# The last block's recurrences at half pace beside a preparation

## The chip, the cores and the metric

The kernel runs on one core of a Trainium2 chip. The metric is device time in microseconds of one execution; a kernel's figure is the median of its runs. A profiled execution gives the trace: PE is TensorE, DVE VectorE, ACT ScalarE, POOL GpSimd, SP the engine that issues most DMAs.

## The reference, cut to what matters

The reference is a network of four blocks on x of 16 x 64 tokens of 256 features, each block with a cross attention into a context of 1024 keys per batch, a sequence layer, and a feed-forward layer, all with a layer norm ahead and a residual sum behind. The change is in the last block (L3), whose three layers are:

```python
# cross attention: 8 heads of 64
q = (x @ Wq).reshape(B, Nq, HEADS, DIM_HEAD)
...
attn = jax.nn.softmax(sim, axis=-1)
...
# state space layer
combined = x @ in_proj_w
u, x_gate = jnp.split(combined, 2, axis=-1)
u_c = conv(u)                                  # 3 taps, by channel
u = jax.nn.silu(u_c + conv_b)
delta, b, c = jnp.split(u @ x_proj_w, ...)
delta = jax.nn.softplus(delta @ dt_proj_w + dt_proj_b)
h = jnp.exp(d_t[:, :, None] * a) * h + d_t[:, :, None] * b_t[:, None, :] * u_t[:, :, None]
y_t = jnp.einsum('bds,bs->bd', h, c_t)         # h: 512 channels x 16 states
...
y = (y + u * D_param) * jax.nn.silu(x_gate)
return y @ out_proj_w
# dense layer: weights of +1 and -1, widths 1024, 1024, 256
h = s0 * _conn_dense(k0, jnp.concatenate([x, -x], axis=-1))
h = s1 * _conn_dense(k1, jax.nn.relu(h) * 2)
return s2 * _conn_dense(k2, jax.nn.relu(h) * 2)
```

(The convolution's call and some shapes are shortened.)

## The kernel before, in words

The 1024 tokens lie as 8 tiles of 128 rows in SBUF (`xs`). The last block, `L3`, weaves three layers together. The attention, `heads64`, goes through 32 steps (tile, batch of the pair, group of four heads) and calls `breathe` four times per step, which in this block is `ssm.go()`. When a tile's attention is added to `xs`, `finished` raises `ssm.ready`. Then the dense layer runs four passes over two tiles each; each pass is a generator whose yields give a share, and `ssm.go(share, hurry=2)` is called at each of them, but for the first two of the first pass. Ahead of each pass stands a loop that calls `go` until those two tiles have come out of the state space layer (`while ssm.done < i + 2`).

The state space layer works on four chunks of 256 tokens (two tiles), each in two generators:

- `prepare(k)`: layer norm, projection (`win`), the convolution's taps on DVE (L1944, L1949), Silu, the b and c rows (`bc`, written to DRAM as `bcs`), delta (L1971 to L1976) and delta times u, written to DRAM as `dus`. It has 14 yields. Some yield `WAIT`, which ends the hurry of that call. A preparation begins when its two tiles have left the attention, and if it is at most two chunks ahead of `done`.
- `items(k)`: the recurrences. There are eight slots (four blocks of 128 channels, two halves), each of four beats. A beat forms the decays on ACT (two activations, L2020), the inputs on DVE (L2026), the recurrence on DVE (L2030, one scan along 512 elements) and the product with c (L2033), in one of six `x` buffers. One beat into the next slot, `add_up` sums the slot's states on PE (L2054, 16 matmul records); every second slot then is multiplied by the gate on DVE (L2060, L2061). After the eight slots come the last sum, the output by `wout` and its sum into `xs` (L89), and `done` rises. So a chunk has 32 beats and three more turns.

`fetch` loads a slot's `rep` buffers (four in all) from `dus`, one slot ahead, in eight DMAs on SP's queue; `bc_rep` (one buffer) comes from `bcs` in eight. The context tiles of the attention and the outputs use SP's queue too.

`go` sets the pace: it resumes the preparation once (or `hurry` times), then adds `share * s.rate` to a credit of at most `2 * s.rate`, and resumes the recurrences once for each whole unit. The rate is 1.1 in the attention and 1.4 in the dense passes. Chunk 0's preparation lies in steps 10 to 13 of the attention, chunk 1's in 18 to 21, chunk 2's in 26 to 29, and chunk 3's in the first dense pass.

The order on PE is the order of the program (`manual_schedule`); on the other engines a scheduler sets it when the program is built, with the tiles' dependences. On each engine instructions run in that order.

Of the kernel before, what the change touches and what calls it, by code (L numbers as in the profile page):

```python
# [42 lines left out]
class Net:  # L43
# [1832 lines left out]
    def state_space(self):  # L1876
# [4 lines left out]
        s = SimpleNamespace(ready=0, done=0, rate=1.1, credit=0.0, prepared=0, started=0)  # L1881
# [183 lines left out]
        def go(share=1.0, hurry=1):  # L2065


            for _ in range(hurry):
                if s.prep is None and s.prepared < NC and s.ready >= 2 * s.prepared + 2 and s.prepared <= s.done // 2 + 1:
                    s.prep = prepare(s.prepared)  # L2070
                got = None if s.prep is None else next(s.prep, s)
                if got is s:
                    s.prepared += s.prep.gi_code is prepare.__code__
                    s.prep = None
                if got is WAIT:
                    break
            if s.work is None and s.started < s.prepared:
                s.work = items(s.started)
                s.started += 1
            self.spare_dve = s.work is not None  # L2080
            s.credit = min(s.credit + share * s.rate, 2 * s.rate)
            while s.work is not None and s.credit >= 1:
                s.credit -= 1
                if next(s.work, s) is s:
                    s.work = None

        def more(i):
            s.ready = i + 1

        s.go, s.more, s.first = go, more, first  # L2090
        s.x = rooms(self.sb, "x", 6)
        s.rep = rooms(self.sb, "rep", 4)
# [333 lines left out]
```

## Time and profile before

| What | us |
|---|---|
| median of 3 runs (lowest, highest) | 2947.67 (2939.41, 2950.96) |
| the profiled execution | 2943.51 |
| its span | 2941.7 |
| PE, DVE, ACT busy in it | 2681.1, 1466.4, 1043.0 |
| 2700 to 2784 (first dense pass): PE, DVE busy | 73.5, 55.4 |
| 2784 to 2834 (second dense pass): PE, DVE busy | 48.3, 44.3 |

The last block's attention begins at about 2017 us and ends at about 2700; the four dense passes fill the rest. The profile's groups name a line, an engine, the output and input tiles, and a count; an instruction issued by a helper bears the helper's line (L69 is the matmul helper, L179 the transpose, L89 the sum into `xs`). A stretch's table gives each engine's busy time within it; its length less PE's busy time is PE's wait.

### The profile page before, as it was taken

To read this page: it belongs to the slowest core of one execution; us is meant where nothing else is said; L and a number is where in the kernel's file an instruction comes from. 1 tells how busy PE (TensorE), PEld (TensorE's weight loads), DVE (VectorE), ACT (ScalarE), POOL (GpSimd) and SP (SyncE) were. 2 spreads that over 40 slices of the span, in tenths; PEclk is the share of its full clock that TensorE was granted. 3 is DMA by queue.
4 is the path that set the end of the run, shared out by engine and by line. 5 is a ranking of instruction groups with operands and counts; after the bars stand their busy time and mean duration, and the time that the engine had idled before them with its cause. 6 is when DMAs were issued, how large, how long until landed. Compare 5 with 4: busy or idle time off the path is not lost. (4 is left out here: it accounts for less than half of the span.)

```text
span 2941.7 us, 42834 instructions
## 1 busy us (share of the span) xinstructions
PE 2681.1 (91%) x16972; PEld 1973.5 (67%) x16972; DVE 1466.4 (50%) x3120; ACT 1043.0 (35%) x2350; POOL 306.1 (10%) x407
## 2 busy tenths in 40 slices
PE   7887898999999898989999998898998898888999
PEld 3556785566666586867777776795766666666777
DVE  2555113666666653234444444323446656658593
ACT  1322121555555441223333322122334455455330
POOL 1111232100000011310101001101001000000000
PEclk9897998999999997989999999899999999999999
DMA  8512772111010113811111111552213213121110
GB/s 235 167 49 81 279 270 73 35 30 36 27 37 23 41 37 137 298 53 45 56 56 45 44 54 61 214 218 75 69 43 87 70 42 94 54 73 29 57 45 8
DMA packets 79221, 253.57 MB, mean 86 GB/s; under 512 B 15151, under 2 KB 26954, under 8 KB 69290
## 3 DMA queue, kind: packets, MB, share of 16 engines
q1 hardware_dynamic: 59562, 165.01, 18.1%
q0 software_dynamic: 13312, 80.28, 8.0%
q10 hardware_dynamic: 6144, 5.51, 0.5%
q8 instruction: 135, 2.21, 0.3%
q14 instruction: 68, 0.56, 0.1%
HBM read 233.80 MB, written 14.82 MB: 85 GB/s over the span
## 5 line engine op out<-in xcount | busy, mean ns | idle before, releaser
L223 DVE TENSOR_REDUCE nmx<-sc 128x1 f32<-128x1024 f32 x264 | 311.9, 1219 | 223.8 <-PE sc L508 132.8
L225 ACT ACTIVATE p<-sc,nmx 128x1024 f32<-128x1024 f32 x264 | 294.6, 1116 | 312.8 <-DVE nmx L223 312.2
L508 PE MATMUL sc<-ctxT,qp 128*128 128x512 f32 (+1 forms) x1024 | 357.0, 603 | 0.0
L508 PEld LDWEIGHTS sc<-ctxT,qp 128*128 128x128 f32 (+1 forms) x1024 | 139.5, 190 | 154.8 <-issue 152.6
L69 PE MATMUL halves<-ctx,pT 128*128 128x192 f32 x1024 | 188.0, 339 | 9.4 <-DVE xs L89 4.0
L69 PEld LDWEIGHTS halves<-ctx,pT 128*128 128x128 f32 x1024 | 175.7, 200 | 12.3 <-DVE xs L89 4.5
L69 PE MATMUL misc<-ctx,pT 128*128 128x192 f32 x1024 | 177.6, 327 | 0.5 <-DVE qT L473 0.5
L235 PE MATMUL ps_t<-ident,p 128*128 128x128 f32 x1088 | 147.6, 278 | 25.2 <-ACT p L225 17.6
L69 PEld LDWEIGHTS misc<-ctx,pT 128*128 128x128 f32 x1024 | 166.3, 191 | 2.2 <-DVE qT L473 1.0
L2020 ACT ACTIVATE da<-rep,al 128x252 f32<-128x252 f32 x256 | 115.1, 498 | 117.8 <-DVE x L2030 101.1
L2030 DVE TENSOR_TENSOR_SCAN x<-da,x 128x512 f32<-128x512 f32 x128 | 152.9, 1220 | 3.4 <-ACT da L2020 2.8
L237 ACT COPY pT<-ps_t 128x512 f32<-128x512 f32 x182 | 104.3, 585 | 140.3 <-PE ps_t L235 138.4
L235 PEld LDWEIGHTS ps_t<-ident,p 128*128 128x128 f32 x1088 | 127.4, 143 | 39.2 <-ACT p L225 22.4
L235 PE MATMUL misc<-ident,p 128*128 128x128 f32 x1024 | 138.3, 280 | 13.4 <-ACT p L225 6.3
L235 PEld LDWEIGHTS misc<-ident,p 128*128 128x128 f32 x1024 | 110.7, 141 | 39.7 <-ACT p L225 14.4
L160 POOL TENSOR_TENSOR ln_rs<-ln_ve,nhalf 128x1 f32<-128x1 f32 x80 | 45.7, 576 | 691.7 <-DVE ln_ve L158 552.7
L237 ACT COPY pT<-misc 128x512 f32<-128x512 f32 x128 | 75.0, 586 | 115.4 <-PE misc L235 115.0
L69 PE MATMUL ps_h<-r,w 128*128 128x256 f32 x512 | 113.4, 381 | 0.0
L69 PE MATMUL gu<-dT,wa 128*128 128x128 f32 (+1 forms) x864 | 104.8, 280 | 3.9 <-ACT dT L64 2.4
L239 DVE COPY pT<-misc 128x512 f32<-128x512 f32 x128 | 88.3, 690 | 38.8 <-PE misc L235 28.2
L69 PEld LDWEIGHTS ps_h<-r,w 128*128 128x128 f32 x512 | 96.6, 190 | 15.9 <-issue 2.5
L69 PEld LDWEIGHTS gu<-dT,wa 128*128 128x128 f32 (+1 forms) x864 | 98.3, 185 | 11.2 <-ACT dT L64 4.8
(478 smaller groups left out, 4479.1 us busy)
## 6 DMA issues: line engine op xcount, KB each, us to landing
ctx<-in_ctx SPq DMA_DIRECT2D x48, 768.0 KB
ctxT<-in_ctxT SPq DMA_DIRECT2D x48, 512.0 KB
w<-in_L2f_W SPq DMA_DIRECT2D x24, 1024.0 KB
rep<-dus SPq DMA_DIRECT2D x256, 64.0 KB
ctxT<-in_ctxT SPq DMA_DIRECT2D x16, 768.0 KB
ctxT<-in_ctxT SPq DMA_DIRECT2D x96, 128.0 KB
ys<-yb ACTq DMA_DIRECT2D x40, 128.0 KB
bc_rep<-bcs SPq DMA_DIRECT2D x32, 128.0 KB
```

Source lines behind the costliest of these rows:

```text
L69: self.nc.tensor.matmul(out, lhsT, rhs, start=n == 0, stop=n == len(pairs) - 1)
L160: nc.gpsimd.tensor_tensor(rs, ve, self.nhalf, ALU.pow)
L223: self.nc.vector.tensor_reduce(nmx, sc, AX.X, ALU.max, negate=True)
L225: self.nc.scalar.activation(p, sc, AF.Exp, bias=nmx, accum_out=sums)
L235: self.nc.tensor.transpose(ps[:, u, :], p[:, at : at + 128], self.ident)
L237: self.nc.scalar.copy(pT[:, 4 * g : 4 * g + 4, :], ps)
L239: self.nc.vector.tensor_copy(pT[:, 0:4, :], ps)
L508: nc.tensor.matmul(sc[u][:, bass.ts(kh, 512)], qp[n][par][rows, h : h + 2, :].rearrange("p h q -> p (h q)"), ctx[0][rows, at], start=n == ...
L2020: nc.scalar.activation(da[:, g, :, 1:], now[j][:, 0, :].rearrange("p (b s) -> p b s", s=S)[:, :, 1:], AF.Exp, scale=al[:, col : col + 1],)
L2030: nc.vector.tensor_tensor_scan(flat, da.rearrange("p g b s -> p (g b s)"), flat, 0.0, ALU.mult, ALU.add)
```

## The change

A call of `go` adds half as much credit while a preparation is in progress, if the rate is at most 1.1. That is so in the attention alone: there a call adds 0.55 in place of 1.1 while `s.prep` is set. The dense passes have rate 1.4, and there a call adds what it added. Nothing else is touched.

```diff
             self.spare_dve = s.work is not None
-            s.credit = min(s.credit + share * s.rate, 2 * s.rate)
+
+            s.credit = min(s.credit + share * s.rate * (1 if s.prep is None or s.rate > 1.1 else 0.5), 2 * s.rate)
             while s.work is not None and s.credit >= 1:
```

From L2082 on the changed kernel's line numbers are one higher.

## The prediction

> **What bounds the kernel now.** I read the page's busy row first: TensorE (PE) is busy for 91% of the span, so what counts is where it waits. The change touches only the last block, so the table of stretches comes next. Its columns are length, then busy time (instructions) of PE, PEld, DVE, ACT and POOL, then granted clock, DMA share and GB/s.
>
> ```profile
> PE 2681.1 (91%) x16972; PEld 1973.5 (67%) x16972; DVE 1466.4 (50%) x3120; ACT 1043.0 (35%) x2350; POOL 306.1 (10%) x407
> ```
>
> ```profile
> 2101.00:2164.00 63.00, 61.92 (x347) 45.91 (x346) 26.87 (x60) 20.03 (x49) 3.77 (x5) 1.00 0.18 55
> 2164.00:2253.00 89.00, 81.23 (x425) 60.40 (x424) 40.86 (x84) 38.04 (x80) 6.81 (x11) 0.98 0.24 68
> 2253.00:2345.00 92.00, 75.85 (x410) 53.83 (x411) 64.02 (x99) 45.06 (x116) 5.53 (x5) 0.93 0.25 73
> 2345.00:2442.00 97.00, 86.42 (x480) 62.04 (x477) 55.76 (x92) 49.15 (x113) 7.43 (x11) 0.98 0.23 65
> 2442.00:2533.00 91.00, 78.18 (x433) 56.35 (x434) 64.23 (x98) 46.78 (x121) 0.55 (x1) 0.96 0.25 74
> 2533.00:2634.00 101.00, 88.79 (x475) 63.23 (x474) 50.71 (x88) 46.37 (x107) 4.65 (x9) 0.95 0.20 59
> ...
> 2834.00:2891.50 57.50, 55.91 (x290) 43.44 (x290) 44.58 (x68) 15.43 (x35) 0.55 (x1) 1.00 0.10 28
> ```
>
> Rows one to six are the attention, four steps each: one with neither preparation nor recurrences, one with a preparation alone, then recurrences alone, both, recurrences alone, both. PE waits 1.1, 7.8, 16.2, 10.6, 12.8 and 12.2 us in them. The last row is the third dense pass with recurrences beside it: PE waits 1.6 of 57.5 us although DVE has 44.6 us of work. So recurrences lie almost free beside the dense layers, and cost PE waits beside the attention.
>
> Then the timeline of DVE where it runs recurrences without interruption, and that of PE around the last dense pass:
>
> ```profile
> 2794.57 2.33 DVE L2030 TENSOR_TENSOR_SCAN x<-da,x 128x512 f32<-128x512 f32 x2
> 2796.82 1.26 DVE L2033 TENSOR_TENSOR x<-x,bc_rep 128x512 f32<-128x512 f32 x2
> 2798.01 1.28 DVE L2026 TENSOR_TENSOR x<-rep,bc_rep 128x512 f32<-128x512 f32 x2
> 2799.21 2.33 DVE L2030 TENSOR_TENSOR_SCAN x<-da,x 128x512 f32<-128x512 f32 x2
> ```
>
> ```profile
> 2877.69 7.17 PE L69 MATMUL halves<-w,r 128*128 128x256 f32 x32
> 2885.44 1.92 PE L2054 MATMUL halves<-x,stack 128*32 128x256 f32 x16 [0.58 <-DVE xs L2159]
> 2887.29 3.72 PE L69 MATMUL halves<-w,ug 128*128 128x256 f32 x16
> ...
> 2895.04 8.86 PE L69 MATMUL ps_h<-hT,w 128*128 128x256 f32 x32 [0.46 <-ACT hT L64]
> ```
>
> A pair of recurrence beats returns after 2799.21 - 2794.57 = 4.64 us: one beat is 2.32 us of DVE. Before the fourth dense pass, PE ends the third (2884.86), sums the last slot (1.92), multiplies by `wout` (3.72), and starts the fourth at 2895.04: nothing of chunk 3's recurrences is left by then.
>
> **The change part by part.** *How many beats move.* A preparation lives for 14 calls of `go` (its 14 yields). Two of them, of chunks 1 and 2, lie in the attention while recurrences run. Each loses 14 x 0.55 = 7.7 beats, 15.4 together. Following the credit call by call, the attention ends with 87 beats done before and 71 after: 16 fewer. Preparation 0 has no recurrence beside it, and preparation 3 falls into the dense passes, at rate 1.4, which the condition leaves alone. Nothing takes the 16 back: in the dense passes the rate is the same, so the lag is carried to the end. Before the fourth pass, the loop that waits for `done` has two beats left in the kernel before (the last sum and the output), and 14 recurrences more after. The built program says the same: after the third pass's two residual updates (now L2160) DVE has 14 triples L2026, L2030, L2033, and PE four sums in a row.
>
> *The tail.* PE has nothing else there. 14 x 2.32 = 32.5 us; the two pairs L2060/L2061 amid them cost 0.40 + 0.34 (from one start to the next at 2840.65) each, 1.5 us. Half of the last sum, 0.96 us, must follow the last beat; it replaces a whole one, 1.92. Together 32.5 + 1.5 + 0.96 - 1.92 = **+33.0**. DVE works in order and the residual updates stand ahead of the 14, so the dense pass's 12.9 us of DVE slack (57.5 - 44.6) is not used for them. What waits behind: both normalizations, the transposes, and the whole fourth pass. Bounds: +24 if four beats are nearer than the order says; +42 if each of the four slots waits some 2 us for its `rep` transfers (eight issues of about 0.4 us and a landing of 1.73 us in the chain make 5 us, within a slot's 9.3, so I take none).
>
> *PE after the gap.* Here a row and a rule differ in size. PE's timeline shows a sum of 2.84 us where others take 1.92, after PE stood 2.60 us:
>
> ```profile
> 2586.89 2.38 PE L69 MATMUL halves<-ug,w 128*32 128x256 f32 x8 [2.60 <-ACT onT L64]
> 2589.71 2.84 PE L2054 MATMUL halves<-x,stack 128*32 128x256 f32 x16 [0.45 <-ACT bc L1962]
> ```
>
> So a pause costs about 0.5 + 0.9 = 1.4 us. The Trainium skill ("TensorE: Matmul & The Clock Gate", Part 1) has the clock at half after an idle window of some 3.4 us, and back after some 3.4 us of work: in the tail PE stands about 7 us between sums, so half a sum and the output (0.96 + 3.72) run at half speed for up to 3.4 us, +1.7. The fourth pass's first layer is slow already (8.86 against 7.17 elsewhere). Row +1.4, rule +1.7, both if the next layer suffers more: I take **+2** (0 to 4).
>
> *The start of the third pass.* Chunk 2's output stood a whole pass ahead of its reader; now it comes one sum before it, in the built order, with chunk 3's first beats among its normalizations. First, L2026 of chunk 3 waits for `bc_rep`, one buffer, free only after chunk 2's last L2033: eight issues of 0.42 us on SP and 1.7 us landing, 5.1 us. L2061, which the output's matmuls need, stands behind that L2026 on DVE. Then four scans (1.13 each), three L2026 and four L2033 (0.6 each) stand ahead of the second normalized tile: 8.7 us. Walking both queues, PE ends the second pass some 12.8 us after chunk 2's last L2033 and gets the third pass's first input at 19.8; less two transposes of 0.4 it waits 6.2 us, where it now waits 2.1 (1.68 and 0.46 before 2834.96). With the clock, **+5** (2 to 8).
>
> *The first and second pass.* One more sum in the second, **+1.85**; the first carries 17 beats instead of 13 on DVE, 9 us more into 28.6 us of its idle time there (2700 to 2784: 84 - 55.4), some of it when PE waits for the preparation: **+1** (-1 to 3).
>
> *What the attention gains.* Four sums leave PE: 4 x 1.85 = **-7.4**, certain, as PE is the bound there. The waits: in the stretches with both, PE waits 10.6 and 12.2 us against 7.8 with a preparation alone, so about seven beats fewer in two of them save some 2 us. In those with recurrences alone it waits 16.2 us for some 17 beats, near 0.9 each; they too lose about seven, because chunk 0's and chunk 1's sums and outputs now fall there, and these bring waits of their own (1.75 us for xs at 2428). I take **-6** (0 to -14). Two outputs of 3.6 us only change their stretch. SP's queue: the slower `rep` loads stand in front of context loads there, but those are two steps ahead; nothing (0 to +3).
>
> *Sum.* 33.0 + 2 + 5 + 1.85 + 1 - 7.4 - 6 = **+29.5**. The profiled execution took 2943.5 us (span 2941.7), so 2973; it lies 4.2 below the median of the runs, 2947.7, from which a new median is 2977.
>
> **The rivals.** (1) *DVE works ahead.* The gap of 14 beats shrinks since DVE's 12.9 us of slack in the third pass swallow five: +29.5 - 11.6 = +18, 2966. For it: the slack is there. Against it: the order of DVE puts the residual updates first.
>
> (2) *The attention is bound by DVE there, and the change pays.* If each of the 16 beats blocked a softmax or an average for its full 2.32 us, the attention would give back 37.1 + 7.4 = 44.5 us against 42.9 lost: 2946; it decides from (42.9 - 7.4) / 16 = 2.2 us per beat. For it: in the second stretch with recurrences alone DVE is busy 64 of 91 us, and PE's waits there end on `on` L522 and `p` L225. Against it: with a preparation beside them, the four steps take 97 and 101 us, with the preparation alone 89; less one output (3.6), 12 to 14 beats cost about 6 us, 0.46 each, which is their sums and no more. All of PE's waits in those two stretches are 22.8 us.
>
> (3) *Transfers pace the tail.* SP loads four `rep` buffers in order, and the third pass's outputs stand among them: at +9 more, 2986.
>
> That the change does nothing is excluded: the built order differs by these beats.
>
> **How the numbers follow.** Forecast 0.72, own range 2964 to 2991; rival 1 0.12, rival 2 0.05, rival 3 0.11. The range of 2958 to 2993 leaves out rival 2 and the ends of the others. A measurement of this kernel tells about 0.5% (15 us) from no change, that is 2962. Slower: all but a few of the forecast's and rival 3's cases and half of rival 1's, 0.88; within: 0.08; faster: most of rival 2, 0.04.
>
> **What would show it.** In the changed kernel: 14 L2030 in a row between the third pass's last residual update and the fourth pass, about 34 us, with PE busy there for four sums only; a wait of 5 to 7 us of PE before the third pass; the attention shorter by 10 to 17 us. It is wrong if PE's waits in the attention fall by over 20 us, if the 14 beats run before the residual updates, or if a slot in the tail takes clearly more than 9.3 us.

## The result and the profile after

The changed kernel takes 2982.43 us (median of 6 runs, 2978.33 to 2985.51) where the kernel before takes 2944.91 (also 6 runs): a ratio of 1.0132, 95% interval 1.0118 to 1.0146, or 37.5 us more. The forecast was 29.5 us more, 2977, in a range of 2958 to 2993. The profiled execution took 2978.33 us, its span 2976.6.

The busy row of the changed kernel's page: the same instructions, PE 18 us busier.

```profile
PE 2699.3 (91%) x16972; PEld 1986.3 (67%) x16972; DVE 1464.7 (49%) x3120; ACT 1042.5 (35%) x2350; POOL 304.7 (10%) x407
```

The table of stretches (length, then busy time and instructions of PE, PEld, DVE, ACT, POOL, granted clock, DMA share, GB/s), of the changed kernel: the four steps beside chunk 1's preparation, the four beside chunk 2's, the third dense pass, and what lies between it and the fourth.

```profile
2356.70:2454.10 97.40, 87.31 (x460) 64.66 (x458) 47.90 (x79) 49.80 (x115) 3.50 (x7) 0.95 0.23 68
2542.30:2635.20 92.90, 81.76 (x426) 60.43 (x425) 49.58 (x79) 48.91 (x112) 3.49 (x7) 0.96 0.19 55
2832.30:2881.60 49.30, 49.28 (x240) 39.71 (x240) 36.46 (x52) 16.17 (x36) 0.00 (x0) 0.97 0.15 41
2881.60:2929.90 48.30, 24.59 (x101) 11.13 (x101) 38.68 (x59) 10.64 (x24) 1.10 (x2) 0.61 0.10 25
```

The same four of the kernel before, cut at the same instructions:

```profile
2360.80:2457.40 96.60, 85.95 (x475) 62.43 (x474) 55.11 (x92) 49.91 (x116) 5.21 (x9) 1.00 0.24 72
2545.90:2647.00 101.10, 88.14 (x458) 63.63 (x457) 57.02 (x89) 50.74 (x117) 2.95 (x6) 0.95 0.22 64
2835.00:2884.90 49.90, 49.86 (x256) 39.40 (x256) 40.84 (x59) 15.05 (x34) 0.00 (x0) 1.00 0.11 29
2884.90:2895.00 10.10, 6.45 (x36) 4.21 (x36) 4.49 (x13) 0.74 (x2) 1.10 (x2) 1.00 0.04 13
```

The last rows are the result: between the third and the fourth pass 10.1 us have become 48.3, with DVE busy for 38.7 of them, and PE's clock at 0.61. The stretch beside chunk 2's preparation is 8.2 us shorter, the one beside chunk 1's 0.8 longer. These two must be read with one thing in mind: in the kernel before, chunk 0's output (3.6 us of PE) lies in the stretch beside chunk 1's preparation and chunk 1's output in the one beside chunk 2's; in the changed kernel each comes one stretch later. Without the outputs, and so for like work, the stretch beside chunk 2's preparation became about 4.6 us shorter, of which one sum less is 1.85, and the one beside chunk 1's about 4.4 us longer.

What happens in the 48.3 us is in PE's timeline of the changed kernel:

```profile
2874.51 7.07 PE L69 MATMUL halves<-w,r 128*128 128x256 f32 x32
2882.15 1.96 PE L2054 MATMUL halves<-x,stack 128*32 128x256 f32 x24 [0.58 <-DVE xs L2160]
2886.71 1.06 PE L2054 MATMUL halves<-x,stack 128*32 128x256 f32 x2 [2.60 <-DVE x L2033]
2890.75 1.91 PE L2054 MATMUL halves<-x,stack 128*32 128x256 f32 x8 [2.98 <-DVE x L2033]
...
2917.88 2.51 PE L2054 MATMUL halves<-x,stack 128*32 128x256 f32 x8 [2.12 <-DVE x L2033]
2920.32 5.52 PE L69 MATMUL halves<-w,ug 128*128 128x256 f32 x16
...
2929.86 8.86 PE L69 MATMUL ps_h<-hT,w 128*128 128x256 f32 x32 [0.46 <-ACT hT L64]
```

PE sums states in pieces and waits at each for DVE's L2033, as a pair of beats ends every 4.64 us. In DVE's own timeline the residual updates stand first, as the order of the built program had it, and then 14 beats follow to 2918.43:

```profile
2881.62 0.48 DVE L2160 SCALAR_TENSOR_TENSOR xs<-halves,sc,xs 128x256 f32<-128x256 f32 x1 [1.27 <-PE halves L69]
2883.24 0.69 DVE L2026 TENSOR_TENSOR x<-rep,bc_rep 128x512 f32<-128x512 f32 x1 [1.14 <-PE halves L2054]
...
2901.98 0.48 DVE L2060 SCALAR_TENSOR_TENSOR v<-ug,vecs,halves 128x256 f32<-128x256 f32 x1 [0.81 <-PE halves L2054]
...
2917.16 1.27 DVE L2033 TENSOR_TENSOR x<-x,bc_rep 128x512 f32<-128x512 f32 x2
```

### The profile page after: what moved, and what is told of

Read it like the earlier page. It is cut to its first block, busy times and chain, and to the rows that moved or that the text cites. A ratio compares the mean times of both kernels' runs of the same rounds, so it can differ in the third digit from the quotient of the medians.

```text
span 2976.6 us, 42824 instructions
## 1 busy us (share of the span) xinstructions
PE 2699.3 (91%) x16972; PEld 1986.3 (67%) x16972; DVE 1464.7 (49%) x3120; ACT 1042.5 (35%) x2350; POOL 304.7 (10%) x407
## 5 line engine op out<-in xcount | busy, mean ns | idle before, releaser
L69 PE MATMUL halves<-ctx,pT 128*128 128x192 f32 x1024 | 194.1, 347 | 14.9 <-ACT du L1972 9.4
L69 PEld LDWEIGHTS halves<-ctx,pT 128*128 128x128 f32 x1024 | 180.8, 205 | 18.9 <-ACT du L1972 10.8
L69 PE MATMUL misc<-ctx,pT 128*128 128x192 f32 x1024 | 177.6, 327 | 0.6 <-DVE qT L473 0.6
L69 PEld LDWEIGHTS misc<-ctx,pT 128*128 128x128 f32 x1024 | 166.3, 191 | 2.2 <-DVE qT L473 1.0
L235 PE MATMUL misc<-ident,p 128*128 128x128 f32 x1024 | 138.3, 280 | 13.4 <-ACT p L225 6.3
L235 PEld LDWEIGHTS ps_t<-ident,p 128*128 128x128 f32 x1088 | 126.7, 142 | 35.2 <-ACT p L225 19.9
L235 PEld LDWEIGHTS misc<-ident,p 128*128 128x128 f32 x1024 | 110.6, 141 | 39.8 <-ACT p L225 14.4
L237 ACT COPY pT<-misc 128x512 f32<-128x512 f32 x128 | 74.9, 585 | 115.6 <-PE misc L235 115.2
L69 PE MATMUL ps_h<-r,w 128*128 128x256 f32 x512 | 113.6, 381 | 0.0
L69 PE MATMUL gu<-dT,wa 128*128 128x128 f32 (+1 forms) x864 | 105.0, 280 | 4.0 <-ACT dT L64 2.4
L69 PEld LDWEIGHTS ps_h<-r,w 128*128 128x128 f32 x512 | 96.6, 190 | 16.1 <-issue 3.3
L69 PEld LDWEIGHTS gu<-dT,wa 128*128 128x128 f32 (+1 forms) x864 | 98.5, 185 | 11.2 <-ACT dT L64 4.8
```

What stands on the lines that cost most here:

```text
L69: self.nc.tensor.matmul(out, lhsT, rhs, start=n == 0, stop=n == len(pairs) - 1)
L235: self.nc.tensor.transpose(ps[:, u, :], p[:, at : at + 128], self.ident)
L237: self.nc.scalar.copy(pT[:, 4 * g : 4 * g + 4, :], ps)
```

## The experiments

Theory A: the beats that the half pace defers are never repaid; they are paid before the fourth pass, where nothing covers them. Rival B: the loss is made by the new interleaving in the attention and the first passes. The other question is what the attention gives back, and why beside one preparation and not beside the other. All edits but two are to the changed kernel. The table cuts the traces at each fourth step's first score matmul, from step 18 on, and at each pass's first matmul; lengths in us. Each row is one execution.

| | beside chunk 1's | four steps alone | beside chunk 2's | last steps | pass 1 | pass 2 | pass 3 and what follows |
|---|---|---|---|---|---|---|---|
| before | 96.6 | 88.5 | 101.1 | 60.8 | 76.3 | 50.8 | 60.1 |
| changed | 97.4 | 88.2 | 92.9 | 61.2 | 78.4 | 57.5 | 97.6 |
| tail's beats left out | 97.5 | 84.1 | 93.3 | 61.2 | 80.2 | 57.5 | 63.6 |
| half beside chunk 1's | 97.4 | 88.2 | 96.2 | 62.0 | 74.9 | 55.3 | 79.3 |
| half beside chunk 2's | 96.6 | 86.0 | 89.0 | 61.0 | 74.4 | 55.3 | 79.1 |
| changed, dense rate 1.8 | 97.4 | 88.1 | 92.9 | 61.2 | 82.5 | 57.8 | 67.0 |
| before, dense rate 1.0 | 96.7 | 88.5 | 101.1 | 60.8 | 69.0 | 52.7 | 90.4 |
| none beside chunk 1's | 93.2 | 88.1 | 98.8 | 59.6 | 79.1 | 59.1 | 97.6 |
| swapped | 102.6 | 90.6 | 99.0 | 66.9 | 76.3 | 51.1 | 60.1 |
| half beside chunk 2's, dense 1.6 | 96.7 | 86.0 | 89.0 | 61.0 | 80.3 | 59.8 | 60.3 |
| none in the delta calls | 94.6 | 76.2 | 101.7 | 60.0 | 81.2 | 53.8 | 73.2 |
| 3/4 beside chunk 2's, dense 1.5 | 96.7 | 88.4 | 92.5 | 61.0 | 72.8 | 56.6 | 60.1 |
| the mixture | 93.0 | 76.2 | 91.8 | 60.3 | 81.4 | 58.8 | 66.1 |

A chunk's output can fall into different stretches in different rows; where a comparison below depends on it, it is said.

### The tail's beats left out

```diff
                 while ssm.done < i + 2:
+                    ssm.left_out = i == NT - 2
                     ssm.go(hurry=2)
...
+                        if s.left_out:
+                            x[half, j] = next_x()
+                            if later is not None and (half, j) == (0, 1):
+                                add_up(k, ug, *later)
+                            yield
+                            continue
                         das.append(das.pop(0))
```

> The changed kernel with the 14 beats that stand between the third and the fourth dense pass left out (their L2020, L2026, L2030, L2033; the sums on PE then read older states). Theory A (the backlog is paid there, in the open): the stretch between the two passes falls from 48.3 us to five sums and an output, about 18, so the time falls by 30, to about 2952; what is left over the kernel before is the sums that PE makes there and shifts in the other passes, less what the attention gained. Rival B (the loss comes from the new interleaving in the attention and the first passes, the wait at the end only shows it): the time falls by less than 15, to 2968 or more.

Measured: 2946.15 us against 2941.12 before, ratio 1.0021 (1.0011 to 1.0030). Against the changed kernel's 1.0132 that is 1.1% of the time, 33 us. The stretch between the passes is 13.4 us in PE's timeline of this run, below the 18 foreseen, as the five sums took 5.5 us together:

```profile
2881.08 5.52 PE L2061 MATMUL halves<-x,stack 128*32 128x256 f32 x80 [0.58 <-DVE xs L2167]
2886.53 3.72 PE L69 MATMUL halves<-w,ug 128*128 128x256 f32 x16
```

Theory A holds, rival B falls: without the 14 beats the kernel is within 0.3% of the one before. (This execution's four steps alone took 84.1 us in place of 88.2; its order in the attention is the changed kernel's, so that is a difference between executions.)

### The dense passes slowed instead, the attention untouched

```diff
-            ssm.rate = 1.4
+            ssm.rate = 1.0
```

(to the kernel before)

> The kernel before, its attention untouched, with rate 1.0 in place of 1.4 in the dense passes: 12 beats are left after the third pass's residual updates. Theory A (beats left before the fourth pass cost DVE's time whatever made them late): that stretch 38.1 - 2 x 2.32 = 33.5 us longer than before, less three sums of 1.85 that leave the first three passes: the kernel before + 28, about 2969. Rival B (the loss is made in the attention): within 10 us of the kernel before.

Measured: 2963.98 us against 2942.22, ratio 1.0088 (1.0064 to 1.0111), 22 us. The attention is the same to 0.1 us, and the third pass with what follows it is 30.3 us longer: a backlog made elsewhere costs the same way. The forecast of 28 was 6 too high; 3 of these are in the third pass and what follows it, for which 33.5 were foreseen. The first pass got 7.3 us shorter: a sum fewer, and chunk 1's output, which now lies in the second pass, are 5.4 of them.

### Half pace beside one preparation only

```diff
-  (1 if s.prep is None or s.rate > 1.1 else 0.5)
+  (1 if s.prep is None or s.rate > 1.1 or s.prepared != 1 else 0.5)
```

> Half pace only beside chunk 1's preparation: 8 beats deferred, 6 of them left before the fourth pass. Theory A: the price of a beat there is 2.32 us, so the stretch before the fourth pass is 38.1 - 8 x 2.32 - 0.8 = 19 us longer than before instead of 38; the attention gains nothing here, as the two traces have that stretch at 96.6 and 97.4: the kernel before + 19 to 22, about 2965. If only the number of deferred beats counted, this and the run with chunk 2 alone would agree within 2 us.

And with `s.prepared != 2`:

> Half pace only beside chunk 2's preparation: also 8 beats deferred and 6 left before the fourth pass. Theory A with the attention's part as the traces have it (that stretch fell from 101.1 to 92.9 us): the kernel before + 19 - 8 = + 11, about 2956. If the gain of 8 us there is not due to the pace beside this preparation but to how the steps happened to fall, it comes out like the run with chunk 1 alone, about 2965.

Measured: 2962.31 us, ratio 1.0077 (1.0059 to 1.0096), for chunk 1; 2949.03, ratio 1.0030 (1.0019 to 1.0041), for chunk 2, against 2941.12. So + 21 and + 8 us (foreseen: 19 to 22 and 11). Both have six beats left, and third passes of 79.3 and 79.1 us, 19 longer than before: the price per beat holds. Of the 13 us between them 11 lie in the attention (343.8 and 332.6 over its four stretches). Beside chunk 2's preparation half pace makes the stretch 12.1 us shorter, 8.5 without chunk 1's output, which left it; beside chunk 1's the stretch is 0.8 us longer although chunk 0's output left it, so about 4.4 longer for like work.

### No beats beside chunk 1's preparation

```diff
-  ... s.prepared != 1 else 0.5)
+  ... s.prepared != 1 else 0)
```

(to the run with half pace beside chunk 1's preparation alone)

> No recurrence beats at all beside chunk 1's preparation, full pace elsewhere: 16 beats deferred and 14 left before the fourth pass, as in the changed kernel. What is asked is why the four steps beside chunk 1's preparation did not get shorter at half pace (96.6 and 97.4 us). If the waits there grow with the beats, they fall to about 87 to 89, as in the steps of chunk 0's preparation, which has no beats beside it. If it is the preparation's own work and a fixed wait, they stay at 95 or more. The time: the kernel before + 38 for the stretch before the fourth pass, less 0 to 9, so + 29 to + 40.

Measured: 2978.97 us against 2942.22, ratio 1.0123 (1.0106 to 1.0140), 37 us. The stretch takes 93.2 us: less than at half pace, but far from the 87 of chunk 0's preparation, between the two cases of the expectation. Against the kernel before it is 3.4 us shorter, and chunk 0's output, which left it, is 3.6: the beats taken away are worth nothing, and the gain does not follow their number. One piece of the trace stands out. The preparation ends before the stretch does, and four beats then run at full pace (from 2415). Behind them PE has its longest wait there, and the 24 matmuls after it take 8.43 us where the kernel before has 5.45:

```profile
2429.30 8.43 PE L69 MATMUL halves<-w,onT 128*128 128x256 f32 x24 [5.19 <-ACT onT L64]
```

### No beats in the delta calls

In the changed kernel PE's timeline beside chunk 1's preparation has this:

```profile
2401.38 1.92 PE L2054 MATMUL halves<-x,stack 128*32 128x256 f32 x16 [1.22 <-ACT du L1972]
...
2417.43 4.16 PE L69 MATMUL halves<-ctx,pT 128*128 128x192 f32 x16 [3.88 <-ACT du L1972]
```

And in ACT's timeline the third L1972 stands behind decays, which wait for recurrences, and behind two exponentials, which wait for maxima that DVE forms only after three recurrences:

```profile
2410.43 0.90 ACT L2020 ACTIVATE da<-rep,al 128x252 f32<-128x252 f32 x2 [1.42 <-DVE x L2030]
2414.67 1.11 ACT L225 ACTIVATE p<-sc,nmx 128x1024 f32<-128x1024 f32 x1 [3.34 <-DVE nmx L223]
...
2416.91 0.47 ACT L1972 ACTIVATE du<-halves,vecs 128x256 f32<-128x256 f32 x1
```

The kernel before has no such wait at L1972 in that stretch: both came with the half pace. This run keeps full pace, but stops the beats in those calls beside chunk 1's preparation:

```diff
             nc.sync.dma_start(self.bcs[k], bc)
+            s.delta = True
             yield
...
                 nc.sync.dma_start(to[c], du[:, c])
+            s.delta = False
             yield
...
-  (1 if s.prep is None or s.rate > 1.1 else 0.5)
+  (0 if s.delta and s.prepared == 1 and s.rate == 1.1 else 1)
```

> Full pace everywhere, but no beats in the five calls of chunk 1's preparation from the b and c rows to the last delta (L1962 to L1972). About five beats are deferred, in the very calls where the changed kernel's trace has PE waiting 3.9 and 1.2 us for the delta activations (L1972), which stand on ACT behind decays (L2020) and softmax exponentials. If these waits are what eats the gain beside chunk 1's preparation at half pace, the four steps take 91 to 94 us, as with no beats at all, in place of 96.6 and 97.4. If not, 96 or more. The time: the kernel before + 12 (four or five beats left before the fourth pass) less that gain: + 7 to + 14.

Measured: 2951.50 us against 2942.33, ratio 1.0026 (1.0010 to 1.0043), 9 us, inside what was expected. The two long waits are gone; PE's waits at L1972 are now those of this line (L1973 here) and one of 0.40:

```profile
2415.12 2.87 PE L69 MATMUL halves<-ctx,pT 128*128 128x192 f32 x16 [1.15 <-ACT du L1973]
```

The stretch takes 94.6 us, just outside the 91 to 94, although chunk 0's output (3.7 us of PE) fell into it, as it does in the kernel before (96.6) and does not in the changed one (97.4). So it is 2.0 us shorter than before with three beats fewer, and about 6.5 shorter than at half pace for like work. But the order is another in the whole stretch, so the run does not set the two waits apart from the rest. What was not expected: the next four steps, at full pace, take 76.2 us in place of 88.5. PE waits 6.5 us there instead of 11.0, its clock is 1.00 instead of 0.96, and it has two sums fewer (3.7 us). The row of the kernel before, then of this run:

```profile
2457.40:2545.90 88.50, 77.48 (x438) 54.60 (x437) 58.25 (x92) 43.22 (x112) 1.70 (x3) 0.96 0.22 63
2456.90:2533.00 76.10, 69.62 (x406) 50.20 (x405) 52.98 (x87) 43.04 (x111) 1.70 (x3) 1.00 0.27 77
```

### The backlog repaid in the dense passes

```diff
-            ssm.rate = 1.4
+            ssm.rate = 1.8
```

> The changed kernel with rate 1.8 in place of 1.4 in the dense passes, which repays the backlog: one turn is left before the fourth pass instead of 15. Theory A: the 38 us before the fourth pass vanish, and the passes with 22, 19 and 22 beats get longer only where DVE has no room (the second: 45.5 us of work in 57.5, six beats or 14 us more): + 5 to 10, so 2945 to 2955. Rival B: the attention's interleaving costs the time, so repaying does not help: 2970 or more.

Measured: 2953.53 us against 2941.12, ratio 1.0046 (1.0029 to 1.0064), 12 us. The third pass and what follows it lose 30.6 of the changed kernel's 97.6 us, and still take 6.9 us more than before, the first pass 6.2. Theory A holds, at the upper end: the room beside the passes was less than assumed.

### The pace swapped

```diff
-  s.credit + share * s.rate
+  s.credit + share * ((1.0 if s.prep is None else 1.4) if s.rate == 1.1 else s.rate)
```

(to the kernel before)

> The kernel before with the pace the other way round: 1.4 per call beside a preparation and 1.0 without one, in the attention; as many beats are done by its end as before. The predicted prices (0.46 us for a beat beside a preparation, about 1.6 where recurrences are alone) make it 5 to 8 us faster. If the stretch beside chunk 2's preparation pays 1.5 us and more for each beat, as its fall by 8 us says, it is 4 to 10 us slower there and gains the like elsewhere: within 5 us of before.

Measured: 2957.48 us against 2942.22, ratio 1.0055 (1.0039 to 1.0072): 15 us slower, outside both expectations. Beside chunk 1's preparation it loses 6.0 us, beside chunk 2's it gains 2.1, and in the last steps, with as many beats on DVE (15) and a sum fewer on PE, it loses 6.1. A price per beat, of either kind, does not describe these stretches.

### Versions meant to beat both

Half pace beside chunk 2's preparation alone and rate 1.6 in the dense passes (the edits above):

> Half pace beside chunk 2's preparation alone, and rate 1.6 in the dense passes, so that one turn is left before the fourth pass as in the kernel before. Theory A: the stretch beside chunk 2's preparation keeps its gain of 8 to 12 us, nothing is left before the fourth pass, and the third pass with 19 beats loses 2 to 4 us: 4 to 8 us faster than the kernel before. If each added beat costs the dense passes what it saves in the attention: the same as before.

Measured: 2938.72 us against 2942.22, ratio 0.9993 (0.9982 to 1.0004): the same. The attention is 14.3 us shorter over its four stretches, and the first two passes lose it again: 4.0 and 9.0 us longer.

Three quarters of the pace, and rate 1.5:

```diff
-  (1 if s.prep is None or s.rate > 1.1 else 0.5)
+  (1 if s.prep is None or s.rate > 1.1 or s.prepared != 2 else 0.75)
...
-            ssm.rate = 1.4
+            ssm.rate = 1.5
```

> Three quarters of the pace beside chunk 2's preparation alone, rate 1.5 in the dense passes: four beats deferred, and by the built order none left before the fourth pass. If the gain of the stretch beside chunk 2's preparation (8 to 12 us at half pace) comes with the first beats taken away and the dense passes take four beats for 3 to 6 us: 3 to 6 us faster than the kernel before. If it falls as the beats do, the dense passes eat it: the same.

Measured: 2933.58 us against 2942.33, ratio 0.9969 (0.9960 to 0.9979): 9 us or 0.3% faster than the kernel before, in 10 runs, and more than the 3 to 6 foreseen. The stretch beside chunk 2's preparation is 8.6 us shorter with chunk 1's output still in it. At half pace it was 8.5 without the output, so in this stretch half of the deferred beats bring the whole gain; over the whole attention they bring 8.4 of 14.4 us. Nothing is left before the fourth pass (60.1 us, as before).

The mixture of this, the stopped delta calls and rate 1.6:

> No beats in the five delta calls beside chunk 1's preparation, three quarters of the pace beside chunk 2's, rate 1.6 in the dense passes; by the built order no beats are left between the third pass's last residual update and chunk 3's output. If the gains add up (14 us over the eight steps from chunk 1's preparation on, 8 beside chunk 2's), less 10 to 14 for the beats in the dense passes: 8 to 12 us faster than the kernel before. If the lengths of the attention's stretches depend on how the waits fall rather than on the beats, they do not add up: within 6 us of the run with three quarters beside chunk 2's preparation alone, either way (2928 to 2940).

Measured: 2934.39 us against 2942.02, ratio 0.9976 (0.9965 to 0.9987). That is 8 us faster, inside the range of the second case (2928 to 2940), but not for its reason: the gains in the attention do add up, to 26 us, and the three passes give back 19, where 10 to 14 were foreseen. The gains do not carry to the end once the passes must take the beats.

## Why the prediction was right, and where it was off

**The beats.** Right. 14 beats stand in the tail, and the credit followed call by call, 87 and 71, gave them. That the first run leaves 5 us of the loss when they are left out, and that the untouched attention with a slower dense rate loses in the same place, shows that the backlog is the cause.

**The tail, forecast + 35 with the clock.** Measured: the third pass and what follows it are 37.5 us longer, of which the stretch between the passes 38.2; the pass itself is 0.6 shorter, as one of its sums moved behind it and its first layer was slower (8.64 us). From the first L2026 to the last L2033 the beats take 35.2 us: the 34.0 of the sum and two waits of DVE for PE's sums (0.81 and 0.19). A third such wait, 1.14 us, stands before the first beat, as its `x` buffer was still to be summed. These two microseconds were missing: the prediction had DVE alone set the pace. The last sum and the clock: from the last L2033 (2918.43) to the output's end (2925.84) 7.4 us pass where the prediction had 0.96 + 3.72, so + 2.7, of which the output, 5.52 us in place of 3.72, is 1.8. The prediction took + 2; that this is near is in part luck, for its picture of the clock was wrong. It had PE standing about 7 us between sums, and the Trainium skill's rule ("TensorE: Matmul & The Clock Gate", Part 1) asks for an idle window of some 3.4 us; PE's longest wait in the tail is 2.98 us, as it sums in pieces, and yet its clock is at half for 37 us on end:

```profile
2887.00:2924.00 37.00, 19.59 (x65) 8.27 (x64) 31.52 (x43) 9.00 (x20) 0.00 (x0) 0.50 0.09 22
```

The fourth pass's first layer is 8.86 us in both. No slot waited for its transfers, so the rival with + 9 had no part.

**The start of the third pass, forecast + 5.** Off: PE waits 2.7 us there (0.47, 1.75 and 0.46) in place of 2.1. The step that failed is the wait for `bc_rep`. SP's timeline has those loads from 2809.11, beside the end of the second pass:

```profile
2809.11 3.56 SPq L2002 DMA_DIRECT2D bc_rep<-bcs  x8
```

DVE had done chunk 2's last beat 6.6 us before PE was ready to sum it, and in that time the loads landed. DVE's last two L2033, and PE's sum:

```profile
2807.81 1.27 DVE L2033 TENSOR_TENSOR x<-x,bc_rep 128x512 f32<-128x512 f32 x2
...
2815.67 1.92 PE L2054 MATMUL halves<-x,stack 128*32 128x256 f32 x16
```

So PE ended the second pass 19.6 us behind that beat, not 12.8, and DVE's part was by then nearly done. The working assumed that DVE is never ahead of PE, in the very pass for which the stretches showed DVE with time to spare. With the slower first layer (1.3 us more) + 1.9 remains.

**The first two passes, forecast + 2.85, as the outputs cancel.** Measured + 2.1 and + 6.6, of which the wait at the third pass is 0.6. So + 8.1 without that wait, where 2.85 were foreseen. An output and a sum more in the second pass are 5.4 of its 6.6; the first pass lost its output (3.6) and is yet 2.1 longer, so it has 5.7 us of new cost. PE waits 7.7 us there (78.4 less 70.7 busy) in place of 3.9. The other 1.9 us are slower matmuls: PE is busy for 1.7 us less, not 3.6, at a granted clock of 0.96 in place of 0.98. The term of + 1 was mis-sized by 4.7. It took DVE's idle time there as room for the beats; the longest of PE's new waits, 2.35 us, is for a result (L2129) to which DVE came at 2764.86, behind beats, while PE's matmuls for it ended at 2760.0. No run set the waits of this pass apart.

**The attention, forecast - 13.4.** Measured - 7.3 over the four stretches from step 18 on (347.0 and 339.7). (The orders part 13 us earlier. Steps 14 to 17 took 97.0 us in place of 95.4, but executions of other runs with the kernel before's order in these steps took 92.6 to 97.4, so nothing is made of this.) The four sums (- 7.4) and the waits (- 6) were both foretold nearly right: PE's waits fell from 10.6, 11.0, 13.0 and 12.0 us to 10.1, 9.4, 11.1 and 9.8, by 6.2 together. What failed is the silent step that the rest of PE's work keeps its speed. PE's busy time fell by 1.1 us only, not 7.4: its matmuls were 6.3 us slower. By the granted clocks of the four rows (1.00, 0.96, 0.95 and 0.94 before, 0.95, 0.94, 0.96 and 0.96 after), PE lost 12.2 us of clock before and 16.3 after: an estimate of about 4 us for the clock's part of the 6.3. The groups of L69 (`ctx`, `pT`) in the stretch beside chunk 1's preparation, first of the kernel before, then of the changed one, show it:

```profile
L69 PE MATMUL halves<-ctx,pT 128*128 128x192 f32 x128 | 22.3, 328 | 2.7 <-DVE xs L89 1.8 <-ACT up L1942 0.9
```

```profile
L69 PE MATMUL halves<-ctx,pT 128*128 128x192 f32 x128 | 26.3, 367 | 5.2 <-ACT du L1972 4.3 <-ACT up L1942 0.9
```

The same 128 records take 26.3 us in place of 22.3, and the stretch's granted clock is 0.95 in place of 1.00. Two of the averages of 16 records make this difference: one takes 4.16 us behind the wait of 3.88 at L1972, and one 5.49, where 2.77 to 2.87 is usual:

```profile
2367.03 0.44 PE L179 MATMUL halves<-ident,on 128*128 128x128 f32 x2 [1.97 <-ACT up L1942]
2368.40 5.49 PE L69 MATMUL halves<-ctx,pT 128*128 128x192 f32 x16 [0.93 <-ACT up L1942]
```

The length of one wait does not decide it. The larger loss stands behind waits of 1.97 and 0.93 us, and in the kernel before a longer one left the clock of the stretch at 1.00:

```profile
2453.24 0.65 PE L235 MATMUL ps_t<-ident,p 128*128 128x128 f32 x4 [2.89 <-DVE qT L473]
```

What sets the clock here is not shown; no run set it apart from the work. Why one preparation gains and the other does not stays open too. The delta waits are a likely part, as the run that takes them away has no slow average left (22.4 us for the 128 records), but the waits for `up` (L1942) before the slowest average are shorter in it as well. And half of the beats gone beside chunk 2's preparation gain 8.5 us for like work, all gone beside chunk 1's nothing.

**The sum.** - 7.3 + 2.1 + 6.6 + 37.5 = + 38.9; the two profiled executions differ by 34.8, as the changed one was 4.1 us ahead at step 18; it was already 5.6 ahead at step 14, where the programs are alike. The tail was forecast within 3 us, and the errors elsewhere, + 6.1 in the attention and + 5.3 in the passes, were partly met by the 4.4 that the third pass's start did not cost in waits. So the number, 8 us short of what was measured, is better than its terms, and two of the signs that the prediction named did not show: the wait before the third pass was 2.7 us and not 5 to 7, the attention 7.3 us shorter and not 10 to 17. The main term, the beats priced by DVE's time before the fourth pass, was right in mechanism and size. The rivals: DVE did not work ahead of the residual updates, and the attention gave back 0.46 us per deferred beat (7.3 / 16), far from the 2.2 at which the change would have paid.

## What to carry to other kernels

A pace that is lowered in one stage and never raised again is a debt, due where the last cover ends: count the units that are left there and price each by the busiest engine's time for one, not by what it cost where it was deferred. Where waits are concerned, compare the clock beside the idle time: PE idled 6.2 us less in the attention here, and its matmuls took 6.3 us more. When a stretch gets shorter, ask first which work left it: an output of 3.6 us, moved to the next stretch, looked like a gain beside one preparation and hid a loss beside the other. And beats moved between stretches do not have a price each; try the move, as the fastest version (3/4 of the pace beside one preparation, repaid under the dense passes) was not the one that the averages pointed to.

## What the runs showed that was not expected

Stretches of the attention mostly have the same length to 0.2 us in different kernels that have the same order of instructions there: 96.6, 96.6, 96.7, 96.7 and 96.7 us beside chunk 1's preparation at full pace, 97.4, 97.4, 97.4 and 97.5 at half pace, 76.2 twice. Most of the differences between kernels there thus come with the order. But there are exceptions with the same order: 84.1 and 88.2 us in the steps alone (the run without the tail's beats and the changed kernel), 93.0 and 94.6 beside chunk 1's preparation (the mixture and the run with the stopped delta calls). So a difference of up to 4 us in a single stretch of a single execution is no proof.

Five sums in a row took 5.52 us where a sum alone is 1.92, with the same 16 records each; no run here shows why.

Executions of the changed kernel and of the others reached step 10 up to 9 us apart (2169.1 to 2178.3 from the span's start), where no edit has had an effect yet.
